# Regrouping the side work of a selective-scan kernel: softplus in three groups, two buffers for delta u, allowances by the kind of state, the first step's prologue alone and an eight-wide last tail

## The chip, the cores and the metric

The kernel runs on one core of a Trainium2 chip. The metric is the device time of one execution in microseconds. All tensors live in HBM at the start and at the end. PE is the matrix engine (PEld its weight loads), DVE the vector engine, ACT the scalar engine, POOL GpSimd, and SP the engine that issues nearly all DMAs. Each engine works through its own queue strictly in order.

## The reference

The input x has 8 images of 64 x 64 positions (L = 4096) with 96 channels. Each image goes through one state-space block, one attention block and one feed-forward block.

```
xz = groupnorm(x, 32 groups) @ in_proj_w.T ; xh, z = split(xz)             # 2 x 192 channels
xc = silu(depthwise_conv3x3(xh) + conv_b)
xs = [xc[diag], xc[anti], reversed(xc[diag]), reversed(xc[anti])]    # K = 4 directions
dts, Bs, Cs = split(einsum(xs, x_proj_weight), [6, 16, 16])
delta = softplus(einsum(dts, dt_projs_weight) + dt_projs_bias)
h[t] = h[t-1] * exp(delta[t] * A[n]) + (delta[t] * u[t]) * B[n, t]   # 16 states n
y[t] = sum over n of h[t] * C[n, t]  (+ D * u)
out  = (layernorm(y back in place) * silu(z)) @ out_proj_w.T, added to x
then: layer norm, linear attention with 6 heads, layer norm,
      feed-forward 96 -> 384 -> 96 in rounded number formats, each added to its input
```

## The kernel before, in words

**The scan.** A step is one image b, one sense q (0 forwards, 1 backwards; two directions lie on the partitions together) and one stretch c of 512 positions: 8 x 2 x 8 = 128 steps. The 192 channels of two directions stand as 128 partitions by G = 3 groups. The main loop in `run` goes over all steps and their 16 states, 2048 iterations i with m, n = divmod(i, 16). Iteration i emits, in this order: `decay(i+2)`, three ACT exponentials (L966); `times_b(i+2)`, for a state of kind "A" eight ACT copies that scale (delta u) transposed by B (L980); `recur(i)`, three DVE scans (L1001), for a state of kind "D" after three DVE products with `du` (L1005); `turn(i+1, part)`, PE transposes of the scaled copies into the three feed banks of PSUM (L988), or for "D" one matmul (L990); `reduce(i-LAG, part)`, PE transposes that add up y over the states (L1036); `keep(i-1)` and `read(i-1)` on POOL, the carry (L1017) and the product of h with C (L1022); `fetch(i+4)`, two SP DMAs that bring a row of C to all partitions (cc, L957). FEED = "DADADADADADAAAAA" gives the kind of each state: D at n = 0, 2, 4, 6, 8, 10, A at the others. LAG is 4, and h has 6 buffers, decay 3, feedT 2, cc 5.

**The prologue** of step m + 2 is started at n = 13 of step m; its input u is brought at n = 8 (L947). It runs 24 matmuls with `wx` on u (L878), copies `rows` (L883), transposes them and writes `x` (L888, L891), and sends C to HBM (`crow`). Then comes softplus as max(v, 0) + ln(1 + exp(-|v|)) with a correction for rounding: matmul and Abs for each group (L901, L903), one Exp (L905) and one Ln (L908) over all three groups, four POOL instructions over all three (L912, L913, L915, L917), per group a second matmul and the DVE correction that adds max(v, 0) (L920, L922). At last POOL forms du = delta * u (L929) into a single buffer, once the D states of the step before have used theirs, and PE and ACT turn it into duT (L934, L936).

**Side work.** Between these, generators carry everything else: `front` of image b + 1 (normalization, convolution L536 and L522, gate, and `walk`, which lays the image out along the diagonals, L581 to L593), `tail` of image b - 1 (`join` for eight chunks: sum of the two directions L640, statistics L650, layer norm, gate, projection, statistics L687, Gram matrix L701 and L706; then attention; then `layers` for eight chunks with statistics L778), and `measures`, the statistics of image b + 2 (L432). A generator yields what it needs next: an engine, an estimated duration, and a lag in iterations. The class `Work` advances them at fixed places of each iteration. Each place adds an allowance to its engine's credit (`PLACES`), and a side task goes ahead while the credit is positive; the prologue's tasks are "urgent" and go first. A task that needs PSUM asks for a bank; during the scan only two banks are free. `finish` emits side work alone, without the scan, until a condition holds: at the start, when a stretch is not yet walked, at every image's start and at the end.

**At the ends.** Before the scan, image 0 goes through measures and front; as soon as its first two stretches are walked, u of steps 0 and 1 are brought, and `finish` runs prologue(0) together with all other side work. After the scan, `tail` of image 7 runs alone, three chunks at a time, with `mid` and `turned` written to HBM by the joins and read back by the layers.

Of the kernel before, what the change touches and what calls it, by code (L numbers as in the profile page):

```python
# [17 lines left out]
P = 128  # L18
HH = WW = 64
L = HH * WW  # L20
DM = 96
# [30 lines left out]
def hybrid_block(ctx, tc, x, out, w):  # L52
# [7 lines left out]
    pool = ctx.enter_context(tc.tile_pool(name="scan", bufs=1))  # L60
    psum = ctx.enter_context(tc.tile_pool(name="psum", bufs=1, space=PSUM))
    with tc.manual_schedule():

        k.tables = lambda: nc.scalar.preload_act_table_set("natural_log_exp_and_others")
        run(tc, pool, psum, dram, x, out, k, NB)


def weights(tc, const, dram, w):
# [60 lines left out]
    logs = tile("logs", [P, ND, NJ])  # L129
    turned = tile("turned", [ND * NJ, P])  # L130

    def loads():

        nc.sync.dma_start(out=logs, in_=w["a_logs"])
# [56 lines left out]
    def layers():  # L191
# [18 lines left out]
        with tc.tile_pool(name="prep", bufs=1, side="right") as prep:  # L210
            w1s = load("w1s", [DM, HID], w["w1"], pool=prep)
            w2s = load("w2s", [P, 3, DM], w["w2"], pool=prep)
            b1s = load("b1s", [P, 3], w["b1"], pool=prep)
# [4 lines left out]

            nc.vector.tensor_copy(k.w1q, w1s, saturate=False)
            nc.vector.tensor_copy(k.w2q, w2s, saturate=False)  # L220
# [44 lines left out]
class Work:  # L265
# [4 lines left out]
    PLACES = {"A": (2.0, 2.5), "V": (1.5, 2.0), "G": (3.5, 5.0), "P": (0.85, 1.2), "S": (9.0, 9.0)}  # L270

    def __init__(self, banks):
        self.now = 0
        self.alone = False
        self.urgent, self.jobs, self.streams = [], [], []
        self.free = [(b, -9) for b in banks]
        self.kept = []
        self.long = []
        self.credit = dict.fromkeys(self.PLACES, 0.0)

    def start(self, gen, urgent=False):
        j = SimpleNamespace(gen=gen, tag="S", us=0.0, bank=False, spin=False, ready=(self.now, 0), done=False)
        self.proceed(j, None, 0)
        (self.urgent if urgent else self.jobs).append(j)
        return j

    def proceed(self, j, given, place):
# [10 lines left out]
        j.ready = (self.now + its, 2 if late else 0) if its or late else (self.now, 0)  # L298

    def bank_for(self, j, place):  # L300
        if j not in self.urgent and not self.alone:
            if any(u.tag == "P" and u.bank for u in self.urgent) or j.bank == "long" and self.long:
                return None
        for i, (b, when) in enumerate(self.free):
            if any(b is x for x in self.kept):
                continue
            if when < self.now or place == 2 or self.alone:
# [12 lines left out]
    def at(self, tag, place=0):  # L320
        gain, most = self.PLACES[tag]
        self.credit[tag] = min(most, self.credit[tag] + gain)
        for j in self.urgent + self.jobs:
            while not j.done and j.tag == tag:
                if j.ready > (self.now, place) and (j.spin or not self.alone):
                    break
                if not self.alone:
                    if self.credit[tag] <= (0.0 if j not in self.urgent else -1.5 if tag == "P" else -99.0):
# [40 lines left out]
    def finish(self, enough):  # L369
# [7 lines left out]
        self.credit = dict.fromkeys(self.PLACES, 0.0)  # L377
# [12 lines left out]
def rsqrt(nc, pool, k, mv, p, n, tag):  # L390

    r = pool.tile([p, n], F32, tag=tag + "r", name=tag + "r")
    s = pool.tile([p, n], F32, tag=tag + "s", name=tag + "s")
    m = pool.tile([p, n], F32, tag=tag + "m", name=tag + "m")
# [14 lines left out]
def fetched(nc, pool, x, b, c):  # L409
    xt = pool.tile([P, 4, DM], F32, tag="xt", name="xt", bufs=2)  # L410
# [57 lines left out]
def front(tc, work, x, k, at, b):  # L468
# [8 lines left out]
    with tc.tile_pool(name=f"f1_{b}", bufs=1, **area) as p1, tc.tile_pool(name=f"f2_{b}", bufs=2, **area) as p2:  # L477
# [17 lines left out]
        def norm(c):  # L495

            xt = fetched(nc, p2, x, b, c)
# [104 lines left out]
def tail(tc, work, x, out, k, at, b):  # L602
# [3 lines left out]
    with tc.tile_pool(name=f"t1_{b}", bufs=1, **area) as p1:  # L606
# [3 lines left out]
        with tc.tile_pool(name=f"t2_{b}", bufs=2, **area) as p2:  # L610

            joined = set()

            def join(c):
                s = slice(4 * c, 4 * c + 4)

                def tile(name, shape, bufs=2):
                    return p2.tile(shape, F32, tag=name, name=name, bufs=bufs)
# [7 lines left out]
                t = tile("t", [P, 4, DM], 3)  # L626
                nc.sync.dma_start(out=t, in_=x[b].rearrange("(t p) c -> p t c", p=P)[:, s, :])
                yield "P", 0.0, 4, False
                while c >= 2 and c - 2 not in joined:
                    yield SPIN  # L630
                gate = tile("gate", [HC, 2, CH])
                nc.sync.dma_start(out=gate, in_=at.gate[:, :, c * CH : (c + 1) * CH])
                st, mv = tile("st", [P, 4, 6]), tile("mv", [P, 4, 2])
                yn = ys[0]
                for j in range(2):
# [12 lines left out]
                    yield dve(1.0, 0)  # L648
# [3 lines left out]
                    work.release(ps)  # L652
                r, m = yield from rsqrt(nc, p2, k, mv, P, 4, "n")
# [3 lines left out]
                yg = tile("yg", [HC, 2, CH])  # L657
# [605 lines left out]
```

## Time and profile before

| what | value |
|---|---|
| median of three runs | 12009.75 us (12005.47 to 12027.36) |
| the profiled execution's own time | 12015.44 us |
| its span, first to last instruction | 12013.6 us |
| up to the first scan | 308.2 us |
| first to last scan | 11319.4 us |
| behind the last scan | 385.8 us |
| busy PE, DVE, ACT, POOL | 9964.7, 9683.0, 9500.1, 9739.2 us |
| mean granted clock of PE | 0.907 |
| DMA | 1213.55 MB, 101 GB/s |

A row of the profile names the line, the engine, the operation, what it writes and reads, and how often; "<-" behind an idle time names what ended it. Matmul ends are modelled, so a busy PE is not PE at its peak. A DVE row such as "h L1001 <- PE feed L988" is time in which DVE stood in front of a scan until PE had filled a feed bank.

### The profile page before, as it was taken

The numbers are of one execution on the slowest core, as the hardware profiler recorded it, in microseconds if no ns is written. First come the engines' busy times: TensorE is split into PE (matmuls) and PEld (weight loads), VectorE is DVE, ScalarE is ACT, GpSimd is POOL, SyncE is SP. The second block draws the span as 40 slices with busy tenths as digits, with TensorE's granted clock in tenths as the row PEclk, the third lists the DMA queues.
The fourth block names the chain that finished last, engine by engine and source line by source line (L and its number), as shares of the span: only waits on it lengthen the run. The fifth ranks groups of instructions, "written<-read, shape, count | busy, mean of one in ns | idle before, by whom it ended". The sixth has DMA issues, their size and how long they took to land.

```text
span 12013.6 us, 186895 instructions
## 1 busy us (share of the span) xinstructions
PE 9964.7 (83%) x62805; PEld 8013.1 (67%) x62805; DVE 9683.0 (81%) x11092; ACT 9500.1 (79%) x19843; POOL 9739.2 (81%) x6927
## 2 busy tenths in 40 slices
PE   5888889888898888888898888988889888888875
PEld 4676677666676667766676666766667666666653
DVE  1888988888888888888888888888888878888971
ACT  2888888878887788887888778887788878878862
POOL 0879988889878888788988888878898888889972
PEclk8999999998999989999899999989899998988985
DMA  3234333533335333343334433343333533322331
GB/s 98 84 97 129 100 91 89 136 106 101 88 96 143 98 93 95 107 125 103 91 92 128 116 93 90 95 129 109 96 92 92 134 105 94 105 83 82 99 96 39
DMA packets 1126629, 1213.55 MB, mean 101 GB/s; under 512 B 453061, under 2 KB 732326, under 8 KB 1125670
## 3 DMA queue, kind: packets, MB, share of 16 engines
q1 hardware_dynamic: 1125670, 1201.61, 36.4%
q8 instruction: 499, 8.18, 0.3%
q14 instruction: 460, 3.77, 0.1%
HBM read 877.99 MB, written 323.14 MB: 100 GB/s over the span
## 4 chain that ended last, share of the span: by engine, by line
PE 30%; ACT 20%; DVE 20%; POOL 12%; issue 9%; DMA 4%; SPq 3%; DVEq 0%; POOLq 0%; ACTq 0%
DVE h L1001 13%; ACT feedT L980 8%; PE y L1036 7%; PE feed L988 7%; POOL h L1022 7%; ACT decay L966 6%; DVE feed L1005 4%; PE bank L536 3%; DMA cc<-crow 2%; PE bank L878 2%; SPq L581 2%; POOL delta L917 1%; PE bank L920 1%; PE feed L990 1%; PE bank L901 1%
## 5 line engine op out<-in xcount | busy, mean ns | idle before, releaser
L1022 POOL TENSOR_TENSOR h<-h,cc 128x1536 f32<-128x1536 f32 x2048 | 7073.5, 3454 | 390.0 <-DMA cc<-crow 197.1
L1001 DVE TENSOR_TENSOR_SCAN h<-decay,carry,feed 128x512 f32<-128x512 f32 x5376 | 6502.6, 1261 | 635.1 <-PE feed L988 528.8
L966 ACT ACTIVATE decay<-delta,a_neg 128x512 f32<-128x512 f32 x6144 | 3976.2, 713 | 1287.5 <-DVE h L1001 1281.8
L988 PE MATMUL feed<-ident,feedT 128*128 128x128 f32 x15360 | 2746.2, 303 | 1502.8 <-DVE h L1001 1211.3
L1036 PE MATMUL y<-ident,h 128*128 128x128 f32 x24576 | 3806.0, 290 | 72.2 <-ACT ys L1064 40.2
L980 ACT ACTIVATE feedT<-duT,rows 128x192 f32<-128x192 f32 x10240 | 3671.1, 443 | 4.5 <-PE feed L988 3.9
L1036 PEld LDWEIGHTS y<-ident,h 128*128 128x128 f32 x24576 | 3151.0, 151 | 530.5 <-issue 477.3
L988 PEld LDWEIGHTS feed<-ident,feedT 128*128 128x128 f32 x15360 | 1972.3, 155 | 2121.2 <-DVE h L1001 663.5
L1005 DVE TENSOR_TENSOR feed<-feed,du 128x512 f32<-128x512 f32 x2304 | 1442.1, 686 | 209.7 <-PE feed L990 205.2
L1017 POOL COPY carry<-h 128x3 f32<-128x3 f32 x2048 | 395.7, 193 | 1072.5 <-DVE h L1001 959.6
L1001 DVE TENSOR_TENSOR_SCAN h<-decay,feed 128x512 f32<-128x512 f32 x768 | 883.3, 1201 | 95.5 <-PE feed L988 80.4
L536 PE MATMUL bank<-wf,xp 97*128 97x192 f32 x4266 | 864.6, 334 | 1.2 <-DVE delta L922 1.2
L990 PE MATMUL feed<-x,pick 77*128 77x512 f32 x1536 | 848.6, 635 | 0.6
L536 PEld LDWEIGHTS bank<-wf,xp 97*128 97x128 f32 x4266 | 696.0, 195 | 29.6 <-issue 18.5
L922 DVE SCALAR_TENSOR_TENSOR delta<-bank,delta 128x512 f32<-128x512 f32 x383 | 259.7, 678 | 280.8 <-POOL delta L917 144.7
L929 POOL TENSOR_TENSOR du<-delta,u 128x1536 f32<-128x1536 f32 x128 | 449.6, 3513 | 36.1 <-DVE delta L922 36.1
L920 PE MATMUL bank<-x,ws 13*128 13x512 f32 x766 | 444.9, 661 | 17.6 <-DVE delta L922 17.6
L915 POOL TENSOR_TENSOR e<-e,duT 128x1536 f32<-128x1536 f32 x128 | 441.7, 3451 | 14.5 <-ACT delta L908 14.4
L901 PE MATMUL bank<-x,ws 13*128 13x512 f32 x764 | 434.1, 648 | 15.0 <-ACT x L891 15.0
L917 POOL TENSOR_TENSOR delta<-delta,e 128x1536 f32<-128x1536 f32 x128 | 441.2, 3447 | 0.1
L912 POOL TENSOR_SCALAR duT<-e 128x1536 f32<-128x1536 f32 x128 | 193.9, 1514 | 227.8 <-ACT e L905 227.8
L990 PEld LDWEIGHTS feed<-x,pick 77*128 77x128 f32 x1536 | 261.4, 202 | 153.7 <-issue 97.7
(263 smaller groups left out, 9059.9 us busy)
## 6 DMA issues: line engine op xcount, KB each, us to landing
cc<-crow SPq DMA_DIRECT2D x4096, 128.0 KB
u<-seq SPq DMA_DIRECT2D x256, 384.0 KB
wide<-ys SPq DMA_DIRECT2D x512, 192.0 KB
ut<-image SPq DMA_DIRECT2D x768, 64.0 KB
seq<-us SPq DMA_DIRECT2D x128, 384.0 KB
part<-ys SPq DMA_DIRECT2D x64, 768.0 KB
y<-part SPq DMA_DIRECT2D x64, 768.0 KB
y<-wide SPq DMA_DIRECT2D x256, 192.0 KB
```

The source lines that it names most:

```text
L536: nc.tensor.matmul(v[:, j, :], flat[:, o : o + P], k.wf[:, i, :], start=(i == 0), stop=(i == 8), skip_group_check=True)
L901: nc.tensor.matmul(ps, w.ws[:, q, g, :], x[0 : 2 * NR + 1, :], start=True, stop=True)
L917: nc.gpsimd.tensor_tensor(delta, delta, e, ALU.add)
L920: nc.tensor.matmul(ps, w.ws[:, q, g, :], x[0 : 2 * NR + 1, :], start=True, stop=True)
L966: nc.scalar.activation(decays[i][:, g, :], made[m].delta[:, g, :], AF.Exp, scale=w.a_neg[:, q, g, n : n + 1])
L980: nc.scalar.activation(f[part], o.duT[part], AF.Copy, scale=scale)
L988: nc.tensor.transpose(feed[g][:, j * P : (j + 1) * P], feeds[i][:, j * G + g, :], w.ident)
L990: nc.tensor.matmul(feed[0], w.pick[:, FEED[:n].count("D"), :], made[m].x, start=True, stop=True)
L1001: nc.vector.tensor_tensor_scan(h[:, g, back], a[:, g, back], feed[g][:, back], init, ALU.mult, ALU.add)
L1005: nc.vector.tensor_tensor(feed[g], feed[0], made[m].du[:, g, :], ALU.mult)
L1022: nc.gpsimd.tensor_tensor(hs[i], hs[i], c.unsqueeze(1).to_broadcast([P, G, T]), ALU.mult)
L1036: nc.tensor.matmul(y[:, j, :], hs[i][:, g, r * P : (r + 1) * P], w.ident, is_transpose=True, start=(n == 0 and j % 4 == 0), stop=(n == NS ...
```

## The change

Seven things change at once. (1) The prologue starts at n = 10 instead of 13, its wx matmuls come in four pieces, and its softplus in three groups that are generators of their own, with POOL's work in pieces of 128 x 512; du has two buffers, rows three. (2) Allowances depend on the kind of the state, two kinds of extra matmuls are charged to PE (`spent`), and urgent work stops at a credit of -1.0 or -0.4. (3) `hurry` emits urgent work alone; it is used for prologue(0), for the start of prologue(1), and in the loop where a step's delta or duT is not there yet. (4) LAG becomes 3 and h gets 5 buffers. (5) Side statistics are emitted one iteration after their ACT copy, and a join's gate is fetched later. (6) There is no `finish` at an image's start; a waiting generator takes its place. (7) The scan's SBUF is given back before the last tail, which runs eight wide, adds the two directions on DVE, and keeps t and xaT in SBUF. The weights' preparation is spread over one stage more.

```diff
-    PLACES = {"A": (2.0, 2.5), "V": (1.5, 2.0), "G": (3.5, 5.0), "P": (0.85, 1.2), "S": (9.0, 9.0)}
+    GAIN = {"A": (2.9, 0.6), "V": (0.5, 2.0), "G": (2.0, 2.0), "P": (1.0, 0.9), "S": (9.0, 9.0)}
+    MOST = {"A": 3.2, "V": 2.2, "G": 2.5, "P": 1.2, "S": 9.0}
...
-    def at(self, tag, place=0):
-        gain, most = self.PLACES[tag]
-        self.credit[tag] = min(most, self.credit[tag] + gain)
-        for j in self.urgent + self.jobs:
+    def spent(self, tag, us):
+        self.credit[tag] -= us
+    def at(self, tag, place=0, kind="D"):
+        self.credit[tag] = min(self.MOST[tag], self.credit[tag] + self.GAIN[tag][kind != "D"])
+        for j in self.urgent + ([] if self.hurried else self.jobs):
...
-                    if self.credit[tag] <= (0.0 if j not in self.urgent else -1.5 if tag == "P" else -99.0):
+                    if self.credit[tag] <= (0.0 if j not in self.urgent else -1.0 if tag == "A" else -0.4):
...
+    def hurry(self, enough):
+        self.alone = self.hurried = True
+        while not enough():
+            self.now += 1
+            for tag, place in (("A", 0), ("V", 0), ("P", 2), ("G", 0)):
+                self.at(tag, place)
+        self.alone = self.hurried = False
...
-                    yield dve(1.0, 0)
+                    yield dve(1.0, 1)
...
-                yield dve(1.7, 0)
+                yield dve(1.7, 1)
...
-            yield [join(c) for c in range(NCH)], 3
+            yield [join(c) for c in range(NCH)], 8 if last else 3
...
+                if last:
+                    t, xaT = kept[c]
...
-        ps = yield bank(1.0, 0)
+        ps = yield bank(0.7, 0)
         v = view(ps, P, TB, NX)
         for j in range(TB):
-            if j == 2:
-                yield pe(0.8)
+            if j:
+                yield pe(0.7)
...
+        while m and not made[m - 1].corrected or m > 1 and not made[m - 2].fed:
+            yield SPIN
         e = tile("e", [P, G, T], 1)
+        o.du = tile("du", [P, G, T])
...
+        def group(g):
             ps = yield bank(0.85)
             nc.tensor.matmul(ps, w.ws[:, q, g, :], x[0 : 2 * NR + 1, :], start=True, stop=True)
             yield act(0.6)
             nc.scalar.activation(e[:, g, :], ps, AF.Abs)
             work.release(ps)
-        nc.scalar.activation(e, e, AF.Exp, scale=-1.0)
-        yield act(1.5, 1)
-        nc.scalar.activation(delta, e, AF.Ln, bias=w.one)
-        yield gp(3.0)
-        nc.gpsimd.tensor_scalar(f, e, 1.0, 1.0, ALU.mult, ALU.add)
-        nc.gpsimd.tensor_scalar(f, f, -1.0, 1.0, ALU.add, ALU.mult)
-        yield gp(3.4, 1)
-        nc.gpsimd.tensor_tensor(e, e, f, ALU.subtract)
-        yield gp(3.4, 1)
-        nc.gpsimd.tensor_tensor(delta, delta, e, ALU.add)
...
+            nc.scalar.activation(e[:, g, :], e[:, g, :], AF.Exp, scale=-1.0)
+            yield act(1.2)
+            nc.scalar.activation(delta[:, g, :], e[:, g, :], AF.Ln, bias=w.one)
+            yield gp(1.05)
+            nc.gpsimd.tensor_scalar(f[:, g], e[:, g], 1.0, 1.0, ALU.mult, ALU.add)
+            nc.gpsimd.tensor_scalar(f[:, g], f[:, g], -1.0, 1.0, ALU.add, ALU.mult)
+            yield gp(1.15)
+            nc.gpsimd.tensor_tensor(e[:, g], e[:, g], f[:, g], ALU.subtract)
+            yield gp(1.15)
+            nc.gpsimd.tensor_tensor(delta[:, g], delta[:, g], e[:, g], ALU.add)
             ps = yield bank(0.85)
             nc.tensor.matmul(ps, w.ws[:, q, g, :], x[0 : 2 * NR + 1, :], start=True, stop=True)
             yield dve(0.7)
             nc.vector.scalar_tensor_tensor(delta[:, g, :], ps, 0.0, delta[:, g, :], ALU.max, ALU.add)
             work.release(ps)
...
-        yield gp(3.4)
-        while m and not made[m - 1].multiplied:
-            yield "G", 0.0, -1, False
-        du = o.du = tile("du", [P, G, T], 1)
-        nc.gpsimd.tensor_tensor(du, delta, u, ALU.mult)
+            yield gp(1.15)
+            nc.gpsimd.tensor_tensor(o.du[:, g], delta[:, g], u[:, g], ALU.mult)
...
-    work.start(prologue(0), urgent=True)
-    work.finish(lambda: not work.urgent)
+    work.start(prologue(0), urgent=0)
+    work.hurry(lambda: hasattr(made[0], "duT"))
...
-    work.start(prologue(1), urgent=True)
+    work.start(prologue(1), urgent=1)
+    work.hurry(lambda: hasattr(made[1], "x"))
...
-    LAG = 4
+    LAG = 3
...
-            if at == LAG + 1 and b:
-                work.finish(all_done)
-                work.stream(between(b))
+            if at == LAG + 1:
+                begun[0] = b
...
-            if n == NS - 3 and m + 2 < len(steps):
-                work.start(prologue(m + 2), urgent=True)
+            if n == 10 and m + 2 < len(steps):
+                work.start(prologue(m + 2), urgent=m + 2)
...
+            work.hurry(lambda: made[(i + 2) // NS].corrected)
             decay(i + 2)
-        work.at("A")
+        work.at("A", 0, FEED[(i + 2) % NS])
         if i + 2 < total:
+            if FEED[(i + 2) % NS] == "A":
+                work.hurry(lambda: hasattr(made[(i + 2) // NS], "duT"))
             times_b(i + 2)
...
-    work.stream(end(NB - 1))
+    work.finish(all_done)
+    scans.close()
...
+    work.stream(tail(tc, work, x, out, w, image(NB - 1), NB - 1, True))
```

## The prediction

> **What bounds the kernel now.** I read the page, then busy times by stage, then VectorE's (DVE's) waits inside the scan, then the order of time at both ends. "n" is the state (0 to 15) within a step; an iteration is one state of one step. From the page:
>
> ```profile
> span 12013.6 us, 186895 instructions
> PE 9964.7 (83%) x62805; PEld 8013.1 (67%) x62805; DVE 9683.0 (81%) x11092; ACT 9500.1 (79%) x19843; POOL 9739.2 (81%) x6927
> ```
>
> Four engines stand between 79% and 83%, so an engine's total decides nothing; the stages do. By stage (window, length, then busy us and count of PE, PEld, DVE, ACT, POOL, PE's granted clock, DMA share, GB/s): one image in the middle and the end, then single steps of 16 states.
>
> ```profile
> 4490.40:5937.90 1447.50, 1230.14 (x7850) 993.53 (x7849) 1209.12 (x1379) 1187.55 (x2481) 1217.77 (x866) 0.92 0.38 105
> 11627.80:12013.60 385.80, 194.86 (x856) 149.44 (x854) 64.14 (x232) 79.97 (x182) 79.02 (x260) 0.59 0.20 54
> ...
> 11258.80:11334.10 75.30, 65.17 (x408) 50.28 (x407) 69.95 (x70) 66.02 (x141) 70.78 (x38) 0.93 0.35 99
> 4749.00:4830.40 81.40, 78.51 (x532) 65.23 (x531) 74.89 (x77) 73.17 (x146) 70.81 (x37) 1.00 0.32 89
> 5279.10:5379.90 100.80, 84.27 (x557) 68.62 (x555) 80.71 (x110) 75.52 (x165) 79.76 (x76) 0.93 0.41 114
> ```
>
> The time is three parts: 308.2 us to the first scan, 11319.4 of scan, 385.8 behind the last scan. In the scan a step without side work takes 75.3, with DVE and POOL at 93% and 94%. A step with side work of the front (convolution, second last row) can take 81.4, with 6.5 of it idle on DVE. A step with joins (last row) takes 100.8, with 20.1 idle on DVE, though no engine is above 84%. So side work is paid mostly in waits. An inner image averages 1447.5 / 16 = 90.5 per step, 15.2 above the bare 75.3: 5.6 of it DVE work (1209.12 / 16 against 69.95), 9.6 further DVE idleness. DVE's waits over the whole scan:
>
> ```profile
> DVE h L1001 <- PE feed L988: 609.2, 479, 9.5
> DVE feed L1005 <- PE feed L990: 201.2, 241, 3.5
> DVE st L650 <- ACT y L647: 159.1, 75, 5.1
> DVE delta L922 <- POOL delta L917: 144.7, 27, 13.6
> DVE delta L922 <- PE bank L920: 122.2, 124, 2.8
> DVE st L687 <- ACT t L683: 103.7, 48, 4.1
> DVE st L778 <- ACT t L774: 87.8, 42, 3.2
> ```
>
> The three "st" rows are side statistics that sit in DVE's queue ahead of a scan and wait for an ACT copy of the same iteration. "delta" is the softplus correction waiting for POOL's 3.45 us lumps. The first row has a known part: the gap ahead of scans is 2.2 us per step at n = 15 and under 0.2 at most n, and this is what stands there in a bare step:
>
> ```profile
> 11324.05 2.80 PE L878 MATMUL bank<-wx,u 128*128 128x77 f32 x24
> 11326.69 0.60 PE L988 MATMUL feed<-ident,feedT 128*128 128x128 f32 x4
> ...
> 11327.40 2.45 DVE L1001 TENSOR_TENSOR_SCAN h<-decay,carry,feed 128x512 f32<-128x512 f32 x2 [2.13 <-PE feed L988]
> ```
>
> PE runs 24 matmuls of the next prologue at once, the transposes for the next scan stand behind them, and DVE idles 2.13.
>
> **The start.** u is in at 224 us and prologue(0) needs PE and ACT, but their in-order queues hold walk transposes that wait for transfers:
>
> ```profile
> 226.00 0.41 ACT L883 COPY rows<-feed 128x308 f32<-128x308 f32 x1 [20.36 <-PE feed L878]
> 227.85 0.71 PEld L588 LDWEIGHTS bank<-ident,ut 128*128 128x128 f32 x4 [2.10 <-issue]
> ...
> 244.58 1.06 PE L888 MATMUL feed<-ident,rows 128*77 128x128 f32 x4
> ...
> 281.21 0.69 DVE L922 SCALAR_TENSOR_TENSOR delta<-feed,delta 128x512 f32<-128x512 f32 x1 [73.26 <-PE feed L920]
> ```
>
> 18 us go between rows and x, and 17 between POOL's last add (264.6) and its correction (281.2). With "hurry" only urgent work is emitted. From 226.4: x 2 us, first group through ACT 2.5, POOL some 14.5, last correction, (delta u) and transposes 6, prologue(1) up to x 4, two decays and the first feed 4: first scan at some 259, a gain of 49. Five walks and eight measures, until now under this wait, go into image 0's scan: 60 transposes (L588) and 32 (L418) at 0.3 us, 15 ACT copies at 0.58, eight statistics at 0.69, and 70 SP issues; but eight steps of that image run nearly bare. I charge 9. **Start: -40** (bounds -10 to -55). The weights load one stage later, ahead of walks that end after it: nothing; a late one would cost its 8 us landing.
>
> **The end.** The joins take 11644 to 11830 in rounds of up to three, then attention some 15 us, then three rounds of layers, each opened by a wait of 17.7, 16.9 and 17.3 us for t<-mid. Eight wide, mid and turned are not written or read back, and there is one round. Loads: the first three joins' y and t landed from 11640.3 to 11653.6, 4.4 us each for 960 KB; with 384 KB of gate 6.2, eight are 50 us. All eight go stage by stage, so DVE's adds hold its queue until the last load: behind it I add some 80 (PE's share of 194.9 at a better clock, and the last join's chain). Layers: POOL 5.5 us a chunk, ACT 5.3, following each other more than overlapping, 95. Sum 17 + 130 + 15 + 95 = 257, **end: -125** (bounds -50, if joins stay at 186; -170, if the stages overlap fully).
>
> **The scan.** (1) Statistics one iteration later: 350.6 us of waits; I take 300 away. (2) Eight-by-three wx matmuls in four pieces of 0.7, charged in full (before 1.8 for 2.8): 2.17 x 128 = 278; I take 195. (3) Softplus by groups, POOL's 3.45 lumps in thirds: of 144.7 I take 70, since each group's add still stands two iterations ahead of its correction. Sum 565. What is late next is the rest of the PE and POOL waits, which bare steps keep too (5.3 idle each), so I let 60% through: -340. (4) Allowances by kind: VectorE's part of a D state is 1.87 + 3.57 = 5.4 and of an A state 3.6, ACT's 1.95 and 4.7; giving side work to ACT in D and to DVE in A evens out what two decay and feedT buffers already smooth. I count it as the reason that the waits do not return, not as a gain.
>
> What it costs. POOL pieces: 128x384 takes 0.914, 128x4 0.20, 128x1536 3.454, so 128x512 lies between 1.20 and 1.28; a scalar piece between 0.50 (a third) and 0.63. Nine and six of them: 13.8 to 15.3 against 13.4 per step, +0.4 to +1.9; I take +1.0, the nearest row being 128x384. Only where POOL is at 94%, in about 20 bare steps, does it show: +20. ACT: Exp 1.486 and Ln 1.562 become three each; 128x512 Exp with a pointer (L966) takes 0.713, so 0 to +1.2 per step, hidden at 88% (66.02 of 75.3). LAG 4 to 3 and h 6 to 5: POOL ends a read by the end of the scan three states later in all but 1.3% of iterations (27), so under 30. No drain at an image's start: states 0 to 5 show no stall there, 0. The u load: brought at n = 8 as before, first used at n = 10, not 13. From its issue to the start of scan n = 11 the median is 10.7 us, one in twenty 2.0 or less; its packets take 5 to 8. PE's other work then stands behind it: 6 steps of 5 us, +30, against 0 if it is hidden and +630 if every step loses one 5 us iteration. (delta u) doubled takes away a wait that the waits show nowhere. **Scan: -340 + 20 + 30 = -290** (bounds -585 and +340).
>
> On the pieces, the Trainium skill, ScalarE: Activation LUTs, section What ACT_TABLE_LOAD costs, speaks against the change: an ACTIVATE has 186 ns fixed and 0.833 ns per element, 93 more for a pointer operand, with 93 overlapped back to back. By it the two rows should be 1.47 and 1.56, as the trace has them, and the split would add an estimated 0.56 us a step, 72 in all if ACT were the bound. The skill's Perfetto Trace Analysis, Optimizing Scalar/DVE Operations, says that larger operations help a saturated engine, while breaking up helps where an unsaturated one causes bubbles on others; the trace has ACT in the second place, and by the first the change would lose.
>
> **Sum.** -40 - 125 - 290 = -455. The profiled execution took 12015.4 (span 12013.6), 5.7 above the median 12009.75 of the three runs; from the median **11555**.
>
> **Rivals.** *Only the ends*: the waits move to the feed rows and the scan stays at 11319: 12010 - 165 = 11845. For it: feed waits are already the largest row; against: the 81.4 us step. Chance 0.19. *The packing works fully*: front steps at 85 (PE 79 at the clock 0.93), join and layer steps at 86 (82.5 of POOL or DVE at 96%), first step 78.7: 1362 per image, -86 x 6, -59 and -10 in images 7 and 0: 12010 - 165 - 585 = 11260. Chance 0.13. *Slower*: the u load. PE waits for it at n = 10 in every step, because SP, which waits for POOL's reads before each cc, issues u an iteration later while POOL does its pieces. It costs one iteration, 5 us, 126 times: 12010 - 455 + 630 = 12185; it decides from 3.6 us per step on. For it: 10.7 against 5 to 8 plus the lag; against: PE has a 4 us iteration in hand there. Chance 0.14. Between it and the first rival, no change: 0.02. That the change does not do what it says (hurry calls stall the scan in each step because groups come too late) would look like the last two; groups start some 13 iterations before they are due.
>
> **Numbers.** Forecast 0.52, and 11400 to 11700 by itself. The range is 11230 to 11900: it holds the first two rivals and leaves out the slower one. Faster by over 0.2% 0.84, within 0.2% 0.02, slower 0.14; 0.2% is what a measurement can tell from no change.
>
> **What would show it.** First scan near 260; last scan to end near 260; "st" rows below 60 us; the gap at n = 15 below 1; join steps near 92, bare ones 75 to 77. Wrong if wx<-u waits for DMA u<-seq above 150 us, if delta<-POOL grows, or if DVE's feed waits pass 900.

## The result, and the profile after

The changed kernel takes 12450.08 us (median of four runs, 12437.87 to 12473.52) against 12016.06 (12005.47 to 12027.36) before: ratio 1.0363, 95% interval 1.0346 to 1.0380. It is slower by 3.6%, where 3.8% faster was forecast. Its profiled execution took 12442.22 us. The page begins:

```profile
span 12440.4 us, 189322 instructions
PE 10329.4 (83%) x62677; PEld 8183.4 (66%) x62677; DVE 9778.3 (79%) x11100; ACT 9594.7 (77%) x20339; POOL 9958.7 (80%) x8207
```

No engine has much more work: POOL 219.5 us, the rest about 95 or, for PE, a lower granted clock (0.874 against 0.907). By stage (length, then busy us and count of PE, PEld, DVE, ACT, POOL, granted clock, DMA share, GB/s): image 3, a step without side work, and the two halves of what follows the last scan:

```profile
5872.00:7314.78 1442.78, 1249.47 (x7470) 986.31 (x7469) 1188.79 (x1323) 1158.24 (x2460) 1222.45 (x1001) 0.87 0.32 90
1295.89:1375.48 79.59, 66.06 (x408) 50.55 (x407) 71.15 (x70) 66.72 (x144) 72.69 (x47) 0.91 0.34 94
12031.60:12198.10 166.50, 62.83 (x274) 41.71 (x272) 25.70 (x81) 43.87 (x87) 46.55 (x119) 0.53 0.13 38
12198.10:12440.40 242.30, 120.56 (x674) 86.98 (x674) 69.27 (x240) 69.35 (x164) 75.12 (x257) 0.63 0.26 53
```

The first scan starts at 258.9 us (308.2 before), the scan takes 11772.6 (11319.4), and 408.9 lie behind it (385.8). The bare step went from 75.3 to 79.6 or more, though DVE's work in it rose by 1.2 only. Behind the last scan the wide tail of image 7 takes 242.3, but it begins 166.5 late: that stretch is the tail of image 6, which was not done when its time was over. DVE's waits in the scan (us, times, longest), then PE's:

```profile
DVE h L1068 <- PE feed L1055: 1270.6, 1006, 32.9
DVE feed L1072 <- PE feed L1057: 268.7, 225, 7.9
```

```profile
PE feed L1055 <- ACT feedT L1047: 318.4, 754, 3.9
PE bank L930 <- DMA u<-seq: 116.0, 23, 23.0
```

The statistics rows fell from 350.6 us to 0.6 inside the scan, and the feed rows took their place: 1270.6 for 609.2. Per step, DVE's gap ahead of scans grew from 5.7 to 11.8 us: 2.79 of the rise stand at n = 11, where u is awaited, 2.35 at the A states n = 1, 3 and 5.

The largest single losses are pauses. In step 14 of images 4, 5 and 6 (143.3, 185.4 and 188.4 us) `bring` finds its stretch not yet walked, and `finish` emits the rest of the convolution alone. In the trace's order of time on DVE, in the last of them:

```profile
10378.88 0.56 DVE L545 COPY pre<-bank 128x384 f32<-128x384 f32 x1 [6.82 <-DMA gate<-z]
...
10414.88 0.36 DVE L545 COPY pre<-bank 128x192 f32<-128x192 f32 x1 [2.37 <-PE bank L559]
...
10455.23 1.28 DVE L1068 TENSOR_TENSOR_SCAN h<-decay,carry,feed 128x512 f32<-128x512 f32 x1 [32.47 <-PE feed L1055]
```

From 10355.5 to 10455 DVE runs one state's scans and otherwise little but the copies of image 7's convolution. The place of the side work tells why: the gate stores of images 1 to 7 begin at 0.30, 1.10, 2.28, 3.41, 4.66, 5.79 and 6.79 images of the scan, before the change at 0.13, 1.11, 2.11 and so on to 6.11. One image's side work needs some 290 iterations where there are 256; nothing halts at an image's start any more, so the delay adds up until a stretch of u is missing. The three pauses, against steps of some 92, cost some 240 us, the leftover 167.

Three edits of the changed kernel are not in the list of seven: PE work that follows work of another engine may be emitted at the second of an iteration's three places for it, no longer only at the third; from the second place on, a PSUM bank released in the same iteration may be given out again; and a waiting prologue keeps banks from side work only once it is ready. The experiments call them the rule for banks.

### The profile page after: what moved, and what is told of

Its sections match the earlier page's. It is cut to its first block, busy times and chain, and to the rows that moved or that the text cites. A ratio compares the mean times of both kernels' runs of the same rounds, so it can differ in the third digit from the quotient of the medians.

```text
span 12440.4 us, 189322 instructions
## 1 busy us (share of the span) xinstructions
PE 10329.4 (83%) x62677; PEld 8183.4 (66%) x62677; DVE 9778.3 (79%) x11100; ACT 9594.7 (77%) x20339; POOL 9958.7 (80%) x8207
## 4 chain that ended last, share of the span: by engine, by line
PE 35%; ACT 28%; DVE 15%; POOL 8%; issue 7%; DMA 5%; SPq 3%; DVEq 0%; POOLq 0%; ACTq 0%
ACT feedT L1047 11%; ACT decay L1032 9%; DVE h L1068 9%; PE y L1101 8%; PE feed L1055 8%; POOL h L1087 5%; DVE feed L1072 4%; PE bank L559 4%; PE bank L930 3%; PE bank L962 2%; PE feed L1057 2%; DMA u<-seq 2%; PE bank L977 2%; SPq L604 1%; ACT duT L997 1%
## 5 line engine op out<-in xcount | busy, mean ns | idle before, releaser
L1101 PE MATMUL y<-ident,h 128*128 128x128 f32 x24576 | 3986.7, 295 | 100.7 <-POOL h L1087 34.4
L1055 PE MATMUL feed<-ident,feedT 128*128 128x128 f32 x15360 | 2857.9, 305 | 1137.6 <-DVE h L1068 722.9
L1101 PEld LDWEIGHTS y<-ident,h 128*128 128x128 f32 x24576 | 3228.9, 154 | 792.3 <-issue 656.7
L930 PE MATMUL bank<-wx,u 128*128 128x77 f32 x3048 | 484.6, 321 | 116.7 <-DMA u<-seq 116.0
L930 PEld LDWEIGHTS bank<-wx,u 128*128 128x128 f32 x3048 | 474.6, 242 | 124.5 <-issue 100.1
L970 POOL TENSOR_SCALAR duT<-e 128x512 f32<-128x512 f32 x384 | 239.0, 623 | 377.9 <-ACT e L966 377.8
L977 PE MATMUL bank<-x,ws 13*128 13x512 f32 x766 | 494.6, 730 | 51.9 <-ACT e L964 47.5
L985 POOL TENSOR_TENSOR du<-delta,u 128x512 f32<-128x512 f32 x384 | 495.6, 1291 | 51.0 <-DVE delta L979 50.9
L973 POOL TENSOR_TENSOR e<-e,duT 128x512 f32<-128x512 f32 x384 | 489.2, 1274 | 30.4
L962 PE MATMUL bank<-x,ws 13*128 13x512 f32 x764 | 484.8, 737 | 33.1 <-ACT e L964 18.1
L975 POOL TENSOR_TENSOR delta<-delta,e 128x512 f32<-128x512 f32 x384 | 492.6, 1283 | 10.7
```

The source lines that it names most:

```text
L930: nc.tensor.matmul(v[:, j, :], u[:, g, j * P : (j + 1) * P], w.wx[:, q, g, :], start=(g == 0), stop=(g == G - 1))
L962: nc.tensor.matmul(ps, w.ws[:, q, g, :], x[0 : 2 * NR + 1, :], start=True, stop=True)
L977: nc.tensor.matmul(ps, w.ws[:, q, g, :], x[0 : 2 * NR + 1, :], start=True, stop=True)
L1055: nc.tensor.transpose(feed[g][:, j * P : (j + 1) * P], feeds[i][:, j * G + g, :], w.ident)
L1101: nc.tensor.matmul(y[:, j, :], hs[i][:, g, r * P : (r + 1) * P], w.ident, is_transpose=True, start=(n == 0 and j % 4 == 0), stop=(n == NS ...
```

## Experiments

Theory at first: this backlog. Rivals: the queues (the late u), and pieces that are dear by themselves. The first three kernels undo one part each, the fourth does one part alone. Times are of one run, where no interval stands; the kernel before took 12014 to 12027 us beside them, and where a kernel was run four times or more, its runs lay 16 to 39 us apart. So a difference of two single runs below some 40 us shows nothing.

**Old allowances** in the changed kernel.

```diff
-    GAIN = {"A": (2.9, 0.6), "V": (0.5, 2.0), "G": (2.0, 2.0), "P": (1.0, 0.9), "S": (9.0, 9.0)}
-    MOST = {"A": 3.2, "V": 2.2, "G": 2.5, "P": 1.2, "S": 9.0}
+    GAIN = {"A": (2.0, 2.0), "V": (1.5, 1.5), "G": (3.5, 3.5), "P": (0.85, 0.85), "S": (9.0, 9.0)}
+    MOST = {"A": 2.5, "V": 2.0, "G": 5.0, "P": 1.2, "S": 9.0}
```

> The changed kernel with the allowances of before (ACT 2.0, DVE 1.5, POOL 3.5, PE 0.85 whatever the kind of the state; caps 2.5, 2.0, 5.0, 1.2), all else as changed. Backlog theory (the side work of one image now needs 1.13 images of scan, which costs the three pauses at step 14 of images 4 to 6, some 240 us, and 166 us of image 6's tail behind the last scan), with the allowances as its reason: the pauses and the leftover go, 11950 to 12100 us. Backlog with the later statistics as its reason: unchanged, 12400 to 12480. Queue theory (most of the loss is PE standing behind the u load and behind late ACT copies in every step): under 100 us either way, 12350 to 12500.

12044.93 us: the pauses are gone, 115 us of leftover remain, an image's side work still needs 1.09 images (before 1.00, changed 1.14).

**Statistics in the iteration of their copy** in the changed kernel.

```diff
-                    yield dve(1.0, 1)
+                    yield dve(1.0, 0)
...
-                yield dve(1.7, 1)
+                yield dve(1.7, 0)
```

> The changed kernel with the side statistics emitted in the iteration of their ACT copy again (lag 0 as before, not 1). Backlog theory with the later statistics as its reason: the side work of an image fits into an image again, the pauses at step 14 go, but some 300 us of DVE waits for ACT copies come back at 60%: 12150 to 12300. Backlog by the allowances, or queue theory: the waits come back and the pauses stay, 12450 to 12650.

12207.25 us: 251 us of statistics waits in the scan are back, and it is faster by 243 all the same. The pauses are gone, and DVE's feed waits fell from 1271 to 948. The work still does not fit: 1.10 images, and 129 us of leftover. An iteration more between copy and statistics is an iteration more in which one of two PSUM banks is held.

**Prologue at n = 13** in the changed kernel.

```diff
-            if n == 10 and m + 2 < len(steps):
+            if n == NS - 3 and m + 2 < len(steps):
```

> The changed kernel with the prologue started at n = 13 as before, not at n = 10. Queue theory: PE's wait for u (116 us in 23 waits) falls under 20, the gap ahead of the scans at n = 11 from 2.9 to under 0.5 us per step, which is 300 us of gaps: 12100 to 12250, with the pauses at step 14 still there. Backlog theory: the waits for u go but only 50 to 120 us come off, 12320 to 12400, for the pauses and the leftover stay.

12041.58 us, below both theories. The gap at n = 11 fell from 2.86 us per step to 0.09, which is 355 us, so the late u was dear by itself. Two of three pauses went too, but 175 us of leftover stay and an image's side work needs 1.11 images. Each of the three parts, then, adds to the backlog, and none makes all of it.

**The kernel before with both ends**: `hurry` for prologue(0), and the wide last tail.

```diff
-    work.finish(lambda: not work.urgent)
+    work.hurry(lambda: hasattr(made[0], "duT"))
...
-    work.stream(end(NB - 1))
+    work.finish(all_done)
+    scans.close()
...
+    work.stream(last_tail(tc, work, x, out, w, image(NB - 1), NB - 1, True))
```

> The kernel before with the first step's prologue emitted alone and the last tail eight wide with the scan's memory given back; the scan and its planner as before. If the two ends are worth what the changed kernel's trace shows (first scan at 258.9 instead of 308.2; last tail alone 242 instead of 386): first scan at 256 to 262, end behind the last scan 235 to 260, scan 11310 to 11360 as five walks and eight measures move into it: 11800 to 11870 us. Rival, that the wide end pays only because image 6's leftover warms it up: end 280 to 330, 11870 to 11950.

11868.26 us (12026.02 before on that chip): first scan at 264.0, end 262.1, scan 11340.4. The ends are worth 158, so it is the scan that fails. This kernel is the base of what follows.

How many iterations an image's side work needs is settled by the order in which the program emits, so it can be counted. Of the next four kernels, the first three were chosen to fit into 256.

**Allowances raised, all else as changed.**

```diff
-    GAIN = {"A": (2.9, 0.6), "V": (0.5, 2.0), "G": (2.0, 2.0), "P": (1.0, 0.9), "S": (9.0, 9.0)}
-    MOST = {"A": 3.2, "V": 2.2, "G": 2.5, "P": 1.2, "S": 9.0}
+    GAIN = {"A": (2.9, 0.6), "V": (0.5, 2.0), "G": (3.5, 3.5), "P": (1.6, 1.6), "S": (9.0, 9.0)}
+    MOST = {"A": 3.2, "V": 2.2, "G": 5.0, "P": 2.0, "S": 9.0}
```

> The changed kernel with six numbers of its allowances raised (P 1.0/0.9 to 1.6/1.6 with a cap of 2.0, G 2.0/2.0 to 3.5/3.5 with a cap of 5.0); all else stays: groups, two delta u, LAG 3, prologue at n = 10, statistics an iteration later, ends. Counted in the order that the program emits, the side work of one image then takes 256 iterations instead of some 290, and nothing is emitted alone inside the scan (507 pieces in the changed kernel). Backlog theory (the slow-down is side work that does not fit into its image): no pauses, no leftover, fewer feed waits: 11600 to 11800, end behind the last scan 240 to 265, scan 11100 to 11280. Density theory (late u, pieces and extra PE charges make steps dear whatever the allowances): only pauses (240) and leftover (166) go: 12040, scan near 11530.

12262.08 us, worse than either theory had it. Pauses and leftover are gone (end 257.3), but the scan is still 11743. The gap at n = 11, 2.99 us per step, is 383 of it; what else makes the steps dear is not told apart here. The backlog is a cause, not the whole.

**The three parts undone together**: the three diffs above in one kernel.

> The changed kernel with the old allowances, the prologue at n = 13 and the statistics in the iteration of their copy, all three. The emitted order then takes 256 iterations per image again, although groups, two delta u, LAG 3 and the wx pieces stay. Backlog theory: close to the kernel before with both ends (11868): 11800 to 11930, with statistics waits of 300 to 350 back and the pauses and the leftover gone. Theory that groups, LAG 3 or h with 5 buffers are dear by themselves: 12000 to 12150, with feed waits above 900.

12187.96 us, above two of the three undone alone. The backlog is gone, and the bare steps at the end of image 0 take 85.4 us instead of 76.2 in the base. So something else makes steps dear, and the bare step shows it:

```profile
1414.21 1.50 ACT L1136 COPY ys<-y 128x768 f32<-128x768 f32 x2 [8.14 <-PE y L1101]
1415.59 1.96 ACT L1032 ACTIVATE decay<-delta,a_neg 128x512 f32<-128x512 f32 x3
1417.44 0.59 ACT L964 ACTIVATE e<-bank 128x512 f32<-128x512 f32 x1
1418.07 0.63 ACT L966 ACTIVATE e<-e 128x512 f32<-128x512 f32 x1
1418.73 0.72 ACT L968 ACTIVATE delta<-e,one 128x512 f32<-128x512 f32 x1
1418.78 0.62 POOL L970 TENSOR_SCALAR duT<-e 128x512 f32<-128x512 f32 x1 [6.49 <-ACT e L966]
1419.36 0.58 ACT L964 ACTIVATE e<-bank 128x512 f32<-128x512 f32 x1
...
1421.26 2.85 ACT L1047 ACTIVATE feedT<-duT,rows 128x192 f32<-128x192 f32 x8
...
1424.75 1.28 DVE L1068 TENSOR_TENSOR_SCAN h<-decay,carry,feed 128x512 f32<-128x512 f32 x1 [3.68 <-PE feed L1055]
```

ACT reaches the copy of the last step's y (ys) 8.14 us before PE has it. Behind it stand the decay and the scaled copies for state 5, and between them two groups of the next softplus. POOL waits 6.49 for that softplus, DVE 3.68 for the feed. ys is copied at n = LAG - 1: with LAG 3 at n = 2, ahead of an A state's copies.

**Later statistics that fit**: the old allowances but for P, n = 13, and

```diff
-                    if self.credit[tag] <= (0.0 if j not in self.urgent else -1.0 if tag == "A" else -0.4):
+                    if self.credit[tag] <= (0.0 if j not in self.urgent else -1.5 if tag == "P" else -99.0):
...
-            work.spent("P", 0.9)
```

> The changed kernel with old allowances for A, V and G, P at 1.3/1.3 with a cap of 1.6, urgent work limited as before, no extra charge to PE, prologue at n = 13; statistics stay one iteration later, and the side work of an image fits into 256 iterations. If the later statistics are worth what I predicted once the work fits (about 300 less 40% that returns elsewhere): 11600 to 11720. If their waits return at the feeds in full: 11830 to 11900, with feed waits of 1000 or more. The same question as in the first kernel, without its prologue at n = 10: between the two lies the price of the early start (0 if the u load is hidden, 100 to 350 if not).

12454.30 us; bare steps 88.9. Both expectations missed, and no run explains this kernel.

**The base with later statistics**, no more.

```diff
-                    yield dve(1.0, 0)
+                    yield dve(1.0, 1)
...
-                yield dve(1.7, 0)
+                yield dve(1.7, 1)
```

> The kernel before with both ends and the statistics one iteration later, nothing else. The emitted order then does not fit: 480 pieces of side work are emitted alone at the images' starts. Backlog theory: the statistics waits (350) go, and halts at n = 4 and 5 of images 1 to 7 cost 25 to 60 us each: 11750 to 11950, no gain or little against 11868. If holding a bank one iteration longer did not slow the side work, there would be no halts and the time would be 11520 to 11650.

11838.55 us. Halts at the image starts appear (step 0 of images 2 to 6 takes 131 to 134 us instead of 79), and the time still does not rise (30 less, which single runs can't tell from nothing).

**LAG 3 and five h buffers on the base.**

```diff
-    LAG = 4
+    LAG = 3
```

> The kernel before with both ends, and LAG 3 with five h buffers; nothing else of the change. New theory, from the trace of the kernel with three parts undone: with LAG 3 the ACT copy of ys stands in ACT's queue at n = 2, ahead of the decay and the scaled copies for state 5, and waits there for PE's last transposes of y (8.1 us in one bare step; ACT ys <- PE y is 701 us in all, against 36 in the kernel before with both ends). LAG theory: ys waits of 500 to 900 us, late steps of image 0 at 82 to 88 instead of 75 to 77, gaps ahead of scans at n = 3 and 5, 12000 to 12250 in all. Groups theory (softplus in three groups is what makes steps dear): 11860 to 11950, ys waits below 150.

11982.54 us, ys waits 279: about half of what the theory had. Bare steps 79.2 to 79.9. The 114 are no clean price of LAG 3: step 0 of images 2 to 6 takes 102 us instead of 79, again halts, and work done in a halt is gone from later steps.

**LAG 4 with five h buffers**, in the changed kernel, in the one of 12454 and in the one of 12188.

```diff
-    LAG = 3
+    LAG = 4
```

> The changed kernel with LAG 4 again, h still with five buffers (six do not fit). LAG theory: ys waits fall from 420 to below 120, the gaps ahead of scans at n = 1, 3 and 5 (0.80, 0.65, 1.92 us per step) to those of the kernel before (0.19, 0.08, 0.75): 12150 to 12300, since the pauses at step 14 and the leftover of image 6 remain (493 pieces are still emitted alone). If five h buffers with LAG 4 make the scan wait for PE's transposes instead, a row h <- PE y appears on DVE and the gain is lost. Groups theory: 12400 to 12480.

> The third kernel of the last four (side work fits into 256 iterations, statistics one iteration later, prologue at n = 13; 12454) with LAG 4. LAG theory: ys waits from 856 to below 120, bare steps from 89 to 76 to 79; the statistics waits stay away: 11550 to 11800. Groups theory: 12300 or more.

> The changed kernel with old allowances, prologue at n = 13, statistics in the iteration of their copy (12188 with LAG 3), and LAG 4. It differs from the kernel before with both ends by the groups, two delta u, wx pieces and five h buffers. LAG theory: 11820 to 11920, ys waits below 120. Groups theory: 12100 or more. What remains above 11868 is the price of the groups, the wx pieces and the five buffers.

14321.17, 14287.07 and 14042.29 us. These tell nothing of LAG: the scan of state i + 5 needs the buffer that PE's transposes of state i still read, and half of the states wait. In the first of them, from 270 to 11900 us:

```profile
DVE h L1068 <- PE y L1101: 2671.8, 1024, 40.5
```

LAG 4 needs six buffers, and with two du and three rows there is no room for them.

**Softplus in groups on the base**: `group` and `turned` of the change, one du, `hurry` in the loop, the rule for banks; LAG 4. Of the edit, the rule:

```diff
-        j.ready = (self.now + its, 2 if late else 0) if its or late else (self.now, 0)
+        j.ready = (self.now + its, 1 if late else 0) if its or late else (self.now, 0)
...
-            if any(u.tag == "P" and u.bank for u in self.urgent) or j.bank == "long" and self.long:
+            if any(u.tag == "P" and u.bank and u.ready <= (self.now, 2) for u in self.urgent) or j.bank == "long" and self.long:
...
-            if when < self.now or place == 2 or self.alone:
+            if when < self.now or place >= 1 or self.alone:
```

> The kernel before with both ends (11868) and softplus in three groups as the change has it, with one delta u as before, and with the changed kernel's rule for giving out PSUM banks (a waiting prologue blocks side work only once it is ready), which the groups need; LAG 4, six h buffers, prologue at n = 13, old allowances, statistics in the same iteration. Groups theory: late steps of image 0 at 80 or more instead of 75 to 77, POOL waits for ACT's Exp in the hundreds of us, 12000 to 12200. Theory that the groups are dear only behind the ys copy of LAG 3: steps at 75 to 79, 11830 to 11950 (154 pieces are emitted alone at the images' starts, some 50 us of it).

12025.38 us, 157 above the base, bare steps 80.5. All three groups are emitted at once: in a bare step ACT's nine pieces run within states 4 to 6, and the correction waits. Its row on DVE, the base first:

```profile
DVE delta L1184 <- POOL delta L1179: 151.9, 30, 13.5
DVE delta L1188 <- POOL delta L1184: 297.4, 127, 6.8
```

The 157 are a sum, not the price of the groups. Five images halt at their start: step 0 of images 2 to 6 takes 90 to 92 us instead of 78 to 79, some 60 in all. Against that stands what the rule for banks gains; it was not run alone.

**The same with LAG 3** and five h buffers.

> The kernel of the run above with LAG 3 and five h buffers: the fourth corner of a square with 11868 (LAG 4, whole), 11982 (LAG 3, whole) and the run above (LAG 4, groups). If the two add, this is the run above plus 114. If they meet (Abs, Exp and Ln of two groups stand behind the ys copy in ACT's queue), it is 200 to 350 above the run above, near the 12188 of the changed kernel with three parts undone, and the gap ahead of scans at n = 5 above 2 us per step.

12057.59 us, 32 more; bare steps 78.9 to 80.0. No image halts at its start here, so that without the 60 of the run above LAG 3 would cost an estimated 90. That is near the 114: the theory that the two meet is not borne out in this form, and not cleanly refuted.

**Later statistics that fit, on the base**: both lags at 1 and the rule for banks as above, without groups, with LAG 4, and

```diff
-    PLACES = {"A": (2.0, 2.5), "V": (1.5, 2.0), "G": (3.5, 5.0), "P": (0.85, 1.2), "S": (9.0, 9.0)}
+    PLACES = {"A": (2.0, 2.5), "V": (1.5, 2.0), "G": (3.5, 5.0), "P": (1.3, 1.6), "S": (9.0, 9.0)}
```

> The kernel before with both ends, statistics one iteration later (11839 with halts of some 52 us at six image starts), P's allowance at 1.3 with a cap of 1.6 and the changed kernel's rule for banks, so that the side work of an image fits into 256 iterations and nothing is emitted alone. No groups, LAG 4, prologue at n = 13. If the predicted gain of the later statistics is there once the work fits: 11838 less 300 to 350 of halts: 11480 to 11620. If denser side work returns as feed waits: 11700 to 11850.

**11491.79 us** against 12014.07: 4.3% below the kernel before, 7.7% below the changed one. The scan takes 10964.8, an inner image 1393, a bare step 75.2. The stage, and DVE's largest wait, the base first:

```profile
4444.00:5837.82 1393.82, 1217.46 (x7832) 977.03 (x7831) 1206.21 (x1377) 1179.88 (x2478) 1215.60 (x864) 0.93 0.39 109
```

```profile
DVE h L1263 <- PE feed L1250: 599.1, 468, 6.4
DVE h L1263 <- PE feed L1250: 680.7, 582, 5.6
```

Less than half of the statistics' waits returned ahead of the scans. DVE's idle time in the scan, all rows together, fell from 1759 us in the base to 1379. These 381 account for the gain of 376. The statistics rows lost 359 of it, the corrections' waits for a PSUM bank 101 (124.9 to 24.3), and the gaps ahead of scans took 154 back (5.64 to 6.84 us per step). DVE is busy for 86.5% of an image, before for 83.5%.

**The same with wx in four pieces.**

```diff
-        ps = yield bank(1.0, 0)
+        ps = yield bank(0.7, 0)
...
-            if j == 2:
-                yield pe(0.8)
+            if j:
+                yield pe(0.7)
```

> The run above with the wx matmuls in four pieces of 0.7. If the gap at n = 14 and 15 (3.1 us per step together) goes as I predicted (195 us): 100 to 200 below the run above. If it moves to other iterations: within 50 of it.

11514.54 us, 23 more, which is no difference for single runs. The gaps at n = 14 and 15 stay (2.33 and 0.95 us per step, without it 2.18 and 0.92). Presumably PE has the same matmuls to do ahead of the same feed; the runs show only that the gap stays.

**The same kernel of 11492 with groups, one iteration apart.**

```diff
         def group(g):
+            if g:
+                yield "P", 0.0, 1 * g, False
             ps = yield bank(0.85)
...
-            yield act(1.2)
+            yield act(1.2, 1)
```

> The kernel of 11492 (both ends, statistics one iteration later, side work that fits, LAG 4, prologue at n = 13) with softplus in groups, the groups started one iteration after each other, and Ln and POOL's last two pieces each one iteration after the piece before (in the changed kernel and in the run with groups alone, 12025, all three groups fall into two or three states). Nothing is emitted alone. Bunching theory (the groups are dear because six us of ACT and fifteen of POOL come at once): late steps of image 0 back to 75 to 76.5 and 11450 to 11560. If the pieces are dear by themselves (1.9 us of POOL and 1.0 of ACT per step): steps of 77 to 81 and 11600 to 11800.

11588.20 us (11583.80 to 11600.24; ratio to before 0.9635, interval 0.9619 to 0.9651). That lies between the two theories. No image halts here, so the 96 us are the price of groups one apart. The last four steps of image 0 take 77.8 us on average, 2.7 more than without groups; bunched, on their base, it was 4.6 more (80.8 for 76.2). The correction's waits are as they were, the kernel of 11492 first:

```profile
DVE delta L1184 <- POOL delta L1179: 99.7, 41, 6.5
DVE delta L1190 <- POOL delta L1186: 96.1, 59, 5.9
```

The price stands elsewhere: the row of scans behind ACT's copy of `rows` rises from 6.9 to 271.4, the feed row falls from 680.7 to 520.9, together 105 more. The gap at n = 15 is 2.85 us per step instead of 0.92, at n = 14 it is 0.51 instead of 2.18.

**The kernel of 11492 with LAG 3 and five h buffers.**

> The kernel of 11492 with LAG 3 and five h buffers; nothing is emitted alone, so this is the price of LAG 3 without the halts that stood in its first run (11982 against 11868). LAG theory: late steps of image 0 at 78 to 80, ys waits above 250 us, 11600 to 11900. If its price was the halts alone: 11480 to 11550.

11660.64 us (11651.41 to 11690.77; ratio 0.9697, interval 0.9682 to 0.9713): LAG 3 costs 169 with no halt about, and ACT's waits for y rise from 61 to 350. ACT in the same bare step, LAG 4 first:

```profile
1353.33 2.86 ACT L1242 ACTIVATE feedT<-duT,rows 128x192 f32<-128x192 f32 x8
1356.09 1.46 ACT L1331 COPY ys<-y 128x768 f32<-128x768 f32 x2
1357.46 3.79 ACT L1228 ACTIVATE decay<-delta,a_neg 128x512 f32<-128x512 f32 x6
```

```profile
1365.30 1.50 ACT L1331 COPY ys<-y 128x768 f32<-128x768 f32 x2 [2.22 <-PE y L1298]
1366.69 1.96 ACT L1228 ACTIVATE decay<-delta,a_neg 128x512 f32<-128x512 f32 x3
1368.54 1.57 ACT L1170 ACTIVATE delta<-e,one 128x1536 f32<-128x1536 f32 x1
1370.01 2.87 ACT L1242 ACTIVATE feedT<-duT,rows 128x192 f32<-128x192 f32 x8
```

With LAG 4 the copies for state 5 are done before ys, which finds its y ready. With LAG 3 ys comes first, waits, and the copies for state 5 start 4.7 us after it: the gap at n = 5 is 1.92 us per step instead of 0.45.

## Why the prediction was wrong, point by point

What failed is the term of the scan: -290 was forecast, and it grew by 453 (11319.4 to 11772.6). Of the prediction's own signs of being wrong, DVE's feed waits passed 900 (1270.6). The waits of wx for u, with 116, stayed under its mark of 150, although the late u cost some 355: most of that stood as the feed waits of DVE.

- **Start, -40**: right for the first scan, which moved by 49.3 (44.2 in the base); image 0 paid some 24 in the base, not 9.
- **End, -125**: right in size (-123.7 in the base), but in the changed kernel 166.5 us of image 6 came in ahead of it.
- **Statistics later, 300, of which 60% stay**: right in kind. With work that fits, the base gains 376, some of it from P's allowance and the rule for banks, which were not tried apart. What failed was the thought that it is free: it holds a bank longer, and alone it already brings halts of 52 us per image.
- **"(4) Allowances by kind ... I count it as the reason that the waits do not return"**: failed. The new numbers are less in sum: ACT 6 x 2.9 + 10 x 0.6 = 23.4 per step instead of 32, POOL 32 instead of 56. I weighed where they put the work, not how much of it they let through. With those of POOL and PE alone raised the work fits, so that ACT's smaller sum was not what kept it from fitting.
- **"No drain at an image's start: states 0 to 5 show no stall there, 0"**: failed. There was none because the work fitted into the 256 iterations. Where it does not fit, the missing halt returns as pauses (240) and leftover (167).
- **LAG, "under 30"**: failed; 169 by the last run. I followed the lag to POOL's reads and not to the other thing that it places, the ACT copy of ys.
- **Groups, -70 of waits and +20 of work**: failed; 96 dearer with the pieces an iteration apart, and 157 as emitted, with halts and the rule for banks in it. That "each group's add still stands two iterations ahead of its correction" does not hold: all three run through within three states.
- **wx in pieces, -195 x 60%**: failed; nothing (+23, within the spread). The gap it started from is also misread: by the trace it is 1.98 us per step at n = 15, not 2.17, with 1.10 more at n = 14.
- **The u load, +30**: failed by size. At n = 11 the gap is 2.86 us per step, 366 in all, between my bounds of 0 and 630. The slower rival named this place; it did not name the rest.
- **Pieces**: POOL's are at my upper bound (+1.9 us per step). On ACT, three Exp of 0.631 and three Ln of 0.722 replace 1.486 and 1.562: +1.01 per step by their durations. But neighbours overlap, and ACT's busy time in the bare step rose by 0.70 (66.02 to 66.72). By the Trainium skill, ScalarE: Activation LUTs, section What ACT_TABLE_LOAD costs, I had estimated 0.56; the single rows agree with its formula within some 3%. Its overlap of 93 ns shows where the next piece reads something else: the Abs at 1419.36 starts 0.09 before the Ln ahead of it ends. Between Abs, Exp and Ln of one group, each of which reads what the one before wrote, there is none (1418.07 + 0.63, then 1418.73). Its Perfetto Trace Analysis, Optimizing Scalar/DVE Operations, has smaller operations help where an unsaturated engine causes bubbles on others. The runs here do not bear it out: bunched, the pieces made more waits (297.4 for 151.9), and an iteration apart they left them as they were (96.1 for 99.7) and cost 96.

The forecast's size was not out of reach: the parts that it counted on most, the ends and the later statistics, give 11492. That this is near the forecast of 11555 is partly luck, for it has an allowance that the forecast did not know and lacks the groups and the wx pieces. Four small terms taken as zero or as gains (drain, allowances, LAG, groups) and the u load turned it.

What stays open: with the side work fitting and the prologue at n = 10, the changed kernel takes 12262. From 11492, the 23 for wx, 169 for LAG 3, 96 for the groups and 383 of gap at n = 11 make 12163, so that some 100 are not accounted for, if the terms add. With the prologue at n = 13 it takes 12454, and the same sum without the gap gives 11780: some 670 are open. The bare step of the three undone together shows groups directly behind the waiting ys. What puts them there was not tried apart; two du, three rows and the later gate are among what remains. The limits on urgent work can't be what makes the 12454, which has the old ones.

## What to carry to other kernels

Where side work is spread over a loop by allowances, count how many iterations a period's work takes before and after an edit: a longer hold of a scarce buffer or a smaller allowance shows nowhere until the work no longer fits, and then as halts in other places. A constant of the pipeline (a lag) is to be followed to everything that it places, and to what stands behind each of these in its engine's queue. Smaller pieces are no gain by themselves: three at once, on an engine that works in order, made the wait behind them longer than one lump at its own place had, and spread out they left it as it was and still cost time.

## Not expected of the hardware

POOL's price per instruction is plain in these sizes: 128x512 products take 1.274 to 1.291 us where 128x1536 take 3.447 to 3.513, so three pieces cost some 11% more than one. The clock granted to PE differs by kernel: 0.922 at 11492 us, 0.919 at 11653, 0.912 at 11868, 0.907 at 12015, 0.874 at 12442 and 0.853 at 14321. It mostly falls as the time grows, but not always: 0.905 at 11839, 0.876 at 12188 and 0.886 at 12262. Why, the runs do not show.
